# Attention's value products: high and low halves of the values in one product, and their sum on VectorE

## The chip, the cores and the metric

The kernel runs on one core of a Trainium2 chip. The metric is the device time of one launch in microseconds, as the median of three runs. A core has five engines that work beside each other, each on its own queue of instructions in order: TensorE (PE, matmuls; its weight loads are shown as PEld), VectorE (DVE), ScalarE (ACT), GpSimd (POOL) and SyncE (SP, which issues DMAs here).

## The reference, cut to what matters

A layer of three parts works on 4096 tokens of 256 channels, in float32: half a mixture-of-experts block, local attention, half a mixture-of-experts block, each behind a layer norm and with a residual.

```python
x = x + 0.5 * ffn(layernorm(x))
x = x + attn(layernorm(x))
x = x + 0.5 * ffn(layernorm(x))
```

The feed-forward part has a shared expert of 2048 hidden units and eight routed ones of 1024, two per token. The attention works in groups of 64 tokens, with 16 heads of 16 channels:

```python
att = softmax(mask(q @ k.T / sqrt(16)))     # per group of 64 tokens and head
y = att @ v                                 # the product that the change touches
out = y @ w_proj
```

## The kernel before, in words

Every float32 operand of a matmul is split into two float16 halves, a high one and a low one (what the rounding left over). A product then is three matmuls: high by high, high by low, low by high. TensorE adds them up in PSUM.

The kernel has four phases. Phase a makes the layer norm and the routing of the first feed-forward block (`tile1`, 32 tiles of 128 tokens) beside the shared expert's first four blocks of 512 tokens. Phase b runs the routed experts. Phase c runs the attention (`tile2`, 32 tiles) beside the remaining shared blocks of the first feed-forward part and most of those of the second. Phase d runs the routed experts of the second part and the last shared block.

In phase c two streams are woven together. The main stream is `shared`: for each of 16 chunks of hidden units, `gate_up` (line 363) makes 6 gate products and 6 up products of 512 columns each, into two PSUM buffers `pgu` out of three. ScalarE takes tanh of the gate (line 370), VectorE combines it with the gate (371) and with the up products (376), ScalarE rounds the result to float16 `hh` (378), and VectorE forms the low half `hl` (379). Line 371 frees the gate's buffer and line 376 the up one. The down products of a chunk (line 389: 8 with `hh`, 4 with `hl`) are issued a chunk later.

The side stream is `attn_tile`, a generator that does one step each time it is asked. `drive` with `RATE_C` = 3.0 and the class `Tiles` with `GAP_C` = 4 decide how many steps fall on each step of the main stream: a new attention tile starts every four slots, so about five are under way at once. The step that this text calls tile j's value step falls into the same slot as tile j+1's step with its scores. The order within each engine's queue is then fixed when the kernel is built: the scheduler lets each engine take the earliest written instruction that is ready on its own model of time. That is why two of a tile's value products can stand ahead of six gate products and the other thirty behind them.

The steps of an attention tile that matter here, for its 128 tokens (two groups g of 64):

- `pqk`, `pv` (line 704): query, key and value products; `vs` (605, 606) holds the values as high and low float16 halves.
- `psc` (641): the scores, 16 products of 64 columns; `S` (644) with the mask added.
- `amx` (650): the row maximum, on VectorE; line 651 subtracts it, on GpSimd, 1024 elements per partition. In the same step ScalarE copies `vs` into `V2` (655), four copies of 64x512, which double-buffers by tile.
- line 659: the exponential; 661 and 662: its high half on ScalarE, its low half on GpSimd; 665: a transposing DMA to `ET`, which has high and low of the exponential one above the other on the 128 partitions.
- the value step, `py` (673): for each g and each of 8 pairs of heads, one product with the high values and one with the low ones, 33 columns each, into the same place of PSUM. Columns 0 to 31 are the values of the pair, column 32 is ones in the high half and zeros in the low one, so that it gives the sum of the exponentials. VectorE takes the reciprocal (676) and multiplies (679), 64 rows at a time, as each half of the rows belongs to one head of the pair.
- `yp` (172 on ScalarE, 173 on GpSimd): `Y` split in two halves; two steps later its transposing DMAs `yt` (691), and two steps after that the output products `pao` (704) and the residual (697). Then comes the next layer norm with logits and, after every fourth tile, the routing.

The small products of the attention (`pqk`, `pv`, `psc`, `py`, `pao`, `pl`, `pp`) share three PSUM buffers. Lines 568 and 569 set the ones and zeros of `V2` once at the start of phase c.

Of the kernel before, what the change touches and what calls it, by code (L numbers as in the profile page):

```python
# [8 lines left out]
F32 = mybir.dt.float32  # L9
F32R = mybir.dt.float32r  # L10
F16 = mybir.dt.float16
# [4 lines left out]
ALU = mybir.AluOpType  # L16
# [4 lines left out]
P = 128  # L21
# [16 lines left out]
class Net:  # L38
# [511 lines left out]
    def attn_init(self, ln_w):  # L550
        nc = self.nc
        a = self.at
        self.lnw = a.tile([P, H], F32, name="lnw")
        nc.sync.dma_start(out=self.lnw, in_=ln_w.unsqueeze(0).to_broadcast([P, H]))
        self.mask = a.tile([P, 64], F32, name="mask")
        m2 = self.sm.tile([P, 64], F32, name="m2", bufs=1)
        for m, base in ((self.mask, 0), (m2, -64)):
            nc.gpsimd.memset(m, 0.0)
            nc.gpsimd.affine_select(
                out=m, in_=m, pattern=[[-1, 64]], compare_op=ALU.is_ge, fill=-3.0e38,  # L560
                base=base, channel_multiplier=1)
        nc.vector.tensor_copy(self.mask[64:P], m2[64:P])
        self.QK = a.tile([P, 24, P], F16, name="QK")
        nc.gpsimd.memset(self.QK, 0.0)
        self.V2 = []
        for i in range(2):
            v = a.tile([P, 2, 2, 8, 34], F16, name=f"V2{i}")
            nc.gpsimd.memset(v[:, :, 0, :, 32:33], 1.0)
            nc.gpsimd.memset(v[:, :, 1, :, 32:33], 0.0)
            self.V2.append(v)  # L570

    def attn_tile(self, R, j, x2, new_fb):

        nc = self.nc
        a = self.at
# [12 lines left out]
        V2 = self.V2[j % 2]  # L588
# [8 lines left out]
        for i in range(2):  # L597
            nc.scalar.activation(qk[:, i, :], pqk[:, i, :], AF.Square, scale=1.0 / XP, accum_out=ss[:, i:i + 1])
        nc.vector.tensor_scalar(
            out=ss, in0=ss, scalar1=XP ** 2 / H, scalar2=1e-6 * XP ** 2, op0=ALU.mult, op1=ALU.add)  # L600
# [6 lines left out]
            out=vs[:, 1, :], in0=pv, scalar=1.0 / XP, in1=vs[:, 0, :], op0=ALU.mult, op1=ALU.subtract)  # L607
        yield
        yield
        for i in range(2):  # L610
            nc.vector.scalar_tensor_tensor(
                out=qk[:, i, :], in0=pqk[:, i, :], scalar=ss[:, i:i + 1], in1=self.lnw,
                op0=ALU.mult, op1=ALU.mult)
        QS = self.QK[:, 0:16].rearrange("p (j s) (r a c) -> p j s r a c", s=2, r=2, a=4)
        for i in range(2):
            if i == 0:
                for r in range(2):
# [5 lines left out]
                        out=s[:, :, 2:4, :], in0=src, in1=s[:, :, 0:2, :], op=ALU.subtract)  # L623
            else:
# [4 lines left out]
                    out=s[:, :, 1::2, :], in0=src, in1=s[:, :, 0::2, :], op=ALU.subtract)  # L629
        yield  # L630
        QT = a.tile([P, 2, 24, 64], F16, name="QT")
        for g in range(2):
            nc.sync.dma_start_transpose(
                out=QT[:, g], in_=self.QK[g * 64:(g + 1) * 64].rearrange("p j c -> p (j c)"))
# [3 lines left out]
        for g in range(2):  # L638
            p = self.m1([P, 8, 64], F32, "psc")
            for jj in range(8):  # L640
                nc.tensor.matmul(  # L641
                    p[:, jj, :], lhsT=QT[:, g, 2 * jj:2 * jj + 2, :].rearrange("p r q -> p (r q)"),
                    rhs=QT[:, g, 16 + jj, :], start=True, stop=True)
            nc.vector.tensor_tensor(  # L644
                out=S[:, g * 8:(g + 1) * 8, :], in0=p,
                in1=self.mask.unsqueeze(1).to_broadcast([P, 8, 64]), op=ALU.add)
        yield
        mx = self.sm.tile([P, 16], F32, name="amx")
        with self.tc.issue_after(self.lows[-2]):
            nc.vector.tensor_reduce(out=mx, in_=S, axis=AX.X, op=ALU.max)  # L650
        self.anchor = nc.gpsimd.tensor_tensor(
            out=S, in0=S, in1=mx.unsqueeze(2).to_broadcast([P, 16, 64]), op=ALU.subtract)
        for g in range(2):
            for d in range(2):
                nc.scalar.copy(  # L655
                    V2[d * 64:(d + 1) * 64, g, :, :, 0:32],
                    vs[g * 64:(g + 1) * 64].rearrange("p l (j c) -> p l j c", c=32))
        yield
        nc.scalar.activation(S, S, AF.Exp, scale=0.25)
# [4 lines left out]
        ET = a.tile([P, 16, P], F16, name="ET")  # L664
        nc.sync.dma_start_transpose(out=ET, in_=e16.rearrange("p h l k -> p (h l k)"))
        yield
        yield
        Y = a.tile([P, 2, 8, 16], F32, name="Y", tag="yy")
        for g in range(2):
            py = self.m1([P, 8, 33], F32, "py")  # L670
            for jj in range(8):
                for l in range(2):
                    nc.tensor.matmul(  # L673
                        py[:, jj, :], lhsT=ET[:, g * 8 + jj, :], rhs=V2[:, g, l, jj, 0:33], start=(l == 0), stop=(l == 1))
            rc = self.sm.tile([P, 8], F32, name="rc")
            nc.vector.reciprocal(rc, py[:, :, 32])
            for r in range(2):
                sl = slice(r * 64, (r + 1) * 64)
                nc.vector.tensor_tensor(
                    out=Y[sl, g], in0=py[sl, :, r * 16:(r + 1) * 16],  # L680
                    in1=rc[sl].unsqueeze(2).to_broadcast([64, 8, 16]), op=ALU.mult)
        yield
        y = self.tok.tile([P, H], F32, name="y")
        nc.sync.dma_start(out=y, in_=R["acc"][j * P:(j + 1) * P])
        yp = a.tile([P, 2 * H], F16, name="yp")
        self.two(yp, Y.rearrange("p g j c -> p (g j c)"), True)
        yield
# [247 lines left out]
```

## Time and profile before

| what | value |
|---|---|
| median of three runs | 1791.72 us (1791.55 to 1791.86) |
| the profiled execution | 1787.42 us |
| its span | 1785.6 us |
| granted TensorE clock | 0.999 |
| value products (line 673) | 1024, from 667.9 to 1267.4 us |
| reciprocals (676) | 64, mean 179 ns |
| multiplications into Y (679) | 128, mean 287 ns |
| copies of the values (655) | 128, mean 616 ns |

The profile is of one execution. The span is the time from its first to its last instruction on the core. In the page and the groups, "128x512 f16<-128x512 f32" gives what is written and what is read, partitions by elements; "x" gives the number of instructions; behind the bar stand busy time, mean duration of one in ns, and the idle time of the engine just before these instructions with what ended it. In the lists in order of time the first number is the start, the second the duration, both in us from the start of the span, and the bracket at the end tells how long the engine had been idle and what it waited for. A matmul's duration contains the time that it takes to pass through the array; the next one starts before it ends.

### The profile page before, as it was taken

The page shows a single profiled execution, that of the slowest core. Times are in us where ns is not written, and L with a number is a line of the kernel's source. Part 1 is how long each engine was busy: PE and PEld are TensorE (multiplying, and loading weights), DVE is VectorE, ACT ScalarE, POOL GpSimd, SP SyncE. Part 2 cuts the span into 40 slices and gives each one's busy share as a digit, 9 for nine tenths or more (in the row PEclk, how much of TensorE's full clock was granted, in tenths as well). Part 3 has the DMA queues.
Part 4 walks back from the last instruction along what each step waited for, and adds up shares of the span by engine and source line. Part 5 has one row for each costly group of instructions (what it writes and reads, how often), then busy time and mean ns, then how long its engine had stood idle before and what let it go on. Part 6 is the DMA issues. An engine that isn't in the chain of part 4 may idle for free.

```text
span 1785.6 us, 37315 instructions
## 1 busy us (share of the span) xinstructions
PE 1771.0 (99%) x13652; PEld 1202.5 (67%) x13652; DVE 1198.5 (67%) x2905; ACT 945.4 (53%) x2053; POOL 757.5 (42%) x1072
## 2 busy tenths in 40 slices
PE   9999999999999999999999999999999999999998
PEld 6666667777777556666666666666666777777765
DVE  7766636666665577787778877788755566666643
ACT  5433325555554356666666666766423455555542
POOL 3777720221111345566776778676430011122210
PEclk9999999999999999999999999999999999999999
DMA  7334133555443245656557576654211144555420
GB/s 218 112 102 120 39 52 103 124 121 117 107 119 75 54 102 96 135 116 142 125 137 143 124 153 122 143 118 114 60 40 34 46 111 110 118 124 118 103 41 13
DMA packets 437544, 185.15 MB, mean 104 GB/s; under 512 B 302193, under 2 KB 434733, under 8 KB 437360
## 3 DMA queue, kind: packets, MB, share of 16 engines
q1 hardware_dynamic: 418880, 160.81, 37.8%
q0 software_dynamic: 17664, 21.17, 6.9%
q8 instruction: 107, 1.75, 0.4%
q10 hardware_dynamic: 816, 0.79, 0.1%
q14 instruction: 77, 0.63, 0.1%
HBM read 78.16 MB, written 42.21 MB: 67 GB/s over the span
## 4 chain that ended last, share of the span: by engine, by line
PE 60%; DVE 2%; ACT 2%; POOL 1%; issue 1%; DMA 1%; SPq 0%; DVEq 0%; POOLq 0%; ACTq 0%
PE pgu L363 36%; PE po L389 18%; PE pqk L704 2%; PE py L673 1%; PE pao L704 1%; PE pv L704 1%; PE psc L641 1%; DVE hl L379 1%; ACT V L655 0%; DVE sl L371 0%; DVE sl L376 0%; ACT hh L378 0%; DMA QT<-QK 0%; DVE S L644 0%; DMA xt<-xa 0%
## 5 line engine op out<-in xcount | busy, mean ns | idle before, releaser
L363 PE MATMUL pgu<-xb,sgu 128*128 128x512 f16 x3072 | 720.2, 380 | 3.4 <-DVE sl L376 2.6
L378 ACT CAST hh<-sl 128x512 f16<-128x512 f32 (+2 forms) x512 | 273.1, 534 | 487.9 <-DVE sl L376 480.6
L363 PE MATMUL pgu<-xe,wc 128*128 128x384 f16 (+1 forms) x3072 | 497.0, 299 | 0.0
L363 PEld LDWEIGHTS <-sgu 128*128 128x128 f16 x3072 | 292.9, 98 | 292.1 <-issue 5.4
L376 DVE SCALAR_TENSOR_TENSOR sl<-pgu,sl 128x512 f32<-128x512 f32 (+2 forms) x512 | 300.9, 588 | 255.0 <-PE pgu L363 228.3
L379 DVE TENSOR_TENSOR hl<-sl,hh 128x512 f16<-128x512 f32 (+2 forms) x512 | 317.4, 620 | 160.3 <-ACT hh L378 157.4
L389 PEld LDWEIGHTS <-hh 128*128 128x128 f16 x3328 | 320.5, 98 | 89.5 <-ACT hh L378 2.1
L363 PEld LDWEIGHTS <-wc 128*128 128x128 f16 x3072 | 300.6, 98 | 92.5 <-issue 0.4
L389 PE MATMUL po<-sdw,hh 128*128 128x256 f16 x2048 | 270.7, 273 | 1.3 <-ACT hh L378 1.3
L515 POOL DMA_INDIRECT out_dram<-eo,eidscatter x40 | 64.3, 1607 | 340.0 <-DVE eo L514 304.5
L374 ACT ACTIVATE sl<-pgu 128x384 f32<-128x384 f32 (+1 forms) x336 | 158.6, 473 | 79.0 <-PE pgu L363 54.5
L389 PE MATMUL po<-wd,hh 128*128 128x256 f16 x1280 | 190.3, 273 | 0.0
L515 POOL DMA_INDIRECT acc<-eo,eidscatter x40 | 65.9, 1648 | 289.7 <-DVE eo L514 253.5
L389 PEld LDWEIGHTS <-hl 128*128 128x128 f16 x1664 | 162.4, 98 | 31.6 <-DVE hl L379 1.8
L371 DVE SCALAR_TENSOR_TENSOR sl<-sl,pgu 128x512 f32<-128x512 f32 x176 | 119.9, 681 | 63.5 <-ACT sl L370 63.0
L389 PE MATMUL po<-sdw,hl 128*128 128x256 f16 x1024 | 156.9, 273 | 1.0 <-DVE hl L379 0.8
L344 POOL DMA_INDIRECT xg<-X,di x128 | 138.3, 1081 | 45.7 <-issue 28.5
L370 ACT ACTIVATE sl<-pgu 128x512 f32<-128x512 f32 x176 | 104.5, 594 | 67.1 <-PE pgu L363 60.5
L106 ACT ACTIVATE wc<-re 128x512 f16<-128x512 f32 x124 | 78.1, 630 | 73.8 <-PE pgu L363 73.7
L389 PE MATMUL po<-wd,hl 128*128 128x256 f16 x640 | 115.2, 273 | 0.0
L107 DVE SCALAR_TENSOR_TENSOR wc<-re,wc 128x512 f16<-128x512 f32 x124 | 85.7, 691 | 13.9 <-ACT wc L106 13.5
L655 ACT COPY V<-vs 64x512 f16<-64x512 f16 x128 | 78.9, 616 | 28.7 <-PE py L673 27.6
(159 smaller groups left out, 1705.4 us busy)
## 6 DMA issues: line engine op xcount, KB each, us to landing
re<-in_L_ffn_rg_dram SPq DMA_DIRECT2D x124, 128.0 KB, 2.3
re<-in_L_ffn_ru_dram SPq DMA_DIRECT2D x124, 128.0 KB, 2.5
re<-in_L_ffn_rd_dram SPq DMA_DIRECT2D x124, 128.0 KB, 2.5
y<-acc SPq DMA_DIRECT2D x64, 128.0 KB, 2.3
y<-in_L_attn_x_dram SPq DMA_DIRECT2D x32, 128.0 KB, 2.0
acc<-xr SPq DMA_DIRECT2D x16, 256.0 KB, 2.3
out_dram<-xr SPq DMA_DIRECT2D x16, 256.0 KB, 5.5
x<-y SPq DMA_DIRECT2D x28, 128.0 KB, 1.9
```

The costliest lines, as they stand in the source:

```text
L107: nc.vector.scalar_tensor_tensor(out=lo, in0=src, scalar=WS, in1=hi, op0=ALU.mult, op1=ALU.subtract)
L344: i = nc.gpsimd.indirect_dma_start(out=R["xg"][:, :], out_offset=bass.IndirectOffsetOnAxis(ap=di[:, t, k:k + 1], axis=0), in_=X, in_offset ...
L363: nc.tensor.matmul(p, lhsT=wc[:, w, i, k, :], rhs=x[:, 2 * a + k, :], start=(j == 0), stop=(j == 5))
L370: self.looks.append(nc.scalar.activation(s, p, AF.Tanh, scale=0.5 / XP).ins)
L371: nc.vector.scalar_tensor_tensor(out=s, in0=s, scalar=1.0, in1=p, op0=ALU.add, op1=ALU.mult)
L374: self.latest[0] = nc.scalar.activation(s, p, AF.Silu, scale=1.0 / XP).ins
L376: self.latest[1] = nc.vector.scalar_tensor_tensor(out=s, in0=ps[1], scalar=1.0 / XP / (2.0 * XP if tanh else 1.0), in1=s, op0=ALU.mult, op ...
L378: nc.scalar.copy(h[0], s)
L379: self.lows.append(nc.vector.tensor_tensor(out=h[1], in0=s, in1=h[0], op=ALU.subtract).ins)
L389: nc.tensor.matmul(outs[t // 2][:, (t % 2) * H:(t % 2 + 1) * H], lhsT=h[a][:, t * P:(t + 1) * P], rhs=wd[:, w], start=(c == 0 and j == 0 a ...
L515: i = nc.gpsimd.indirect_dma_start(out=R["acc"][:, :], out_offset=bass.IndirectOffsetOnAxis(ap=ids[:, t:t + 1], axis=0), in_=eo, in_offset ...
L655: nc.scalar.copy(V2[d * 64:(d + 1) * 64, g, :, :, 0:32], vs[g * 64:(g + 1) * 64].rearrange("p l (j c) -> p l j c", c=32))
```

## The change

For seven of the eight pairs of heads, high and low values now lie side by side in `V2`, so that one product of 66 columns multiplies both. Columns 0 to 32 of a pair hold the high part and the sum, columns 34 to 65 the low part. The eighth pair keeps its two products, of 33 and 32 columns, added up in PSUM[...]. ScalarE copies the low parts of the seven pairs to `yl` in SBUF; the eighth place of `yl` is zero from the start. VectorE takes the reciprocals, adds the high part from PSUM and the low part from `yl` into `Y`, and multiplies `Y` of both groups by the reciprocals in one operation at the end. A tile has 18 value products in place of 32, two more ScalarE copies, and one more VectorE operation.

```diff
@@ attn_init
-            v = a.tile([P, 2, 2, 8, 34], F16, name=f"V2{i}")
-            nc.gpsimd.memset(v[:, :, 0, :, 32:33], 1.0)
-            nc.gpsimd.memset(v[:, :, 1, :, 32:33], 0.0)
+            v = a.tile([P, 2, 8, 2, 34], F16, name=f"V2{i}")
+            nc.gpsimd.memset(v[:, :, :, :, 32:34], 0.0)
+            nc.gpsimd.memset(v[:, :, :, 0, 32:33], 1.0)
             self.V2.append(v)
+        self.yl = [a.tile([P, 8, 32], F32, name=f"yl{g}") for g in range(2)]
+        for t in self.yl:
+            nc.gpsimd.memset(t[:, 7], 0.0)
@@ attn_tile
                 nc.scalar.copy(
-                    V2[d * 64:(d + 1) * 64, g, :, :, 0:32],
+                    V2[d * 64:(d + 1) * 64, g, :, :, 0:32].rearrange("p j l c -> p l j c"),
                     vs[g * 64:(g + 1) * 64].rearrange("p l (j c) -> p l j c", c=32))
@@ attn_tile
         Y = a.tile([P, 2, 8, 16], F32, name="Y", tag="yy")
+        rc = self.sm.tile([P, 2, 8], F32, name="rc")
         for g in range(2):
-            py = self.m1([P, 8, 33], F32, "py")
-            for jj in range(8):
-                for l in range(2):
-                    nc.tensor.matmul(
-                        py[:, jj, :], lhsT=ET[:, g * 8 + jj, :], rhs=V2[:, g, l, jj, 0:33], start=(l == 0), stop=(l == 1))
-            rc = self.sm.tile([P, 8], F32, name="rc")
-            nc.vector.reciprocal(rc, py[:, :, 32])
+            py = self.m1([P, 512], F32, "py")
+            for jj in range(7):
+                nc.tensor.matmul(
+                    py[:, jj * 66:(jj + 1) * 66], lhsT=ET[:, g * 8 + jj, :],
+                    rhs=V2[:, g, jj].rearrange("p l c -> p (l c)")[:, 0:66], start=True, stop=True)
+            for l in range(2):
+                n = 33 - l
+                nc.tensor.matmul(
+                    py[:, 462:462 + n], lhsT=ET[:, g * 8 + 7, :], rhs=V2[:, g, 7, l, 0:n], start=(l == 0), stop=(l == 1),
+                    skip_group_check=True)
+            yl = self.yl[g]
+            nc.scalar.copy(yl[:, 0:7], py[:, 0:462].rearrange("p (j c) -> p j c", c=66)[:, :, 34:66])
+            hi = py[:, 0:495]
+            hi = bass.AP(hi.tensor, hi.offset, [hi.ap[0], [66, 8], [1, 33]])
+            nc.vector.reciprocal(rc[:, g], hi[:, :, 32])
             for r in range(2):
                 sl = slice(r * 64, (r + 1) * 64)
-                nc.vector.tensor_tensor(
-                    out=Y[sl, g], in0=py[sl, :, r * 16:(r + 1) * 16],
-                    in1=rc[sl].unsqueeze(2).to_broadcast([64, 8, 16]), op=ALU.mult)
+                c = slice(r * 16, (r + 1) * 16)
+                nc.vector.tensor_tensor(out=Y[sl, g], in0=hi[sl, :, c], in1=yl[sl, :, c], op=ALU.add)
+        nc.vector.tensor_tensor(
+            out=Y, in0=Y, in1=rc.unsqueeze(3).to_broadcast([P, 2, 8, 16]), op=ALU.mult)
```

## The prediction

> **What bounds the kernel now.** I read the page's first part, then the table by stage, the groups of instructions inside the attention stage, and last the instructions in order of time around one attention tile.
>
> The page, busy time of each engine:
> ```profile
> PE 1771.0 (99%) x13652; PEld 1202.5 (67%) x13652; DVE 1198.5 (67%) x2905; ACT 945.4 (53%) x2053; POOL 757.5 (42%) x1072
> ```
> A busy TensorE proves little here, since the ends of its matmuls are modelled. What counts is whether it ever waits. The value products run from 667.9 to 1267.4 us, so I took four consecutive attention tiles of that stretch (columns: length, then busy time of each engine, clock, DMA):
> ```profile
> core 0: us, PE busy (x) PEld busy (x) DVE busy (x) ACT busy (x) POOL busy (x), PEclk, DMA share, GB/s
> 1034.30:1112.80 78.50, 78.50 (x671) 50.25 (x670) 62.89 (x164) 53.15 (x112) 58.72 (x81) 1.00 0.68 136
> ```
> A tile takes 78.5/4 = 19.6 us. VectorE is busy 80% of it, ScalarE 68%, GpSimd 75%, at full clock. The groups of 745 to 1245 us (last column: idle time of the engine before them):
> ```profile
> L363 PE MATMUL pgu<-xb,sgu 128*128 128x512 f16 x1230 | 289.0, 379 | 0.0
> L379 DVE TENSOR_TENSOR hl<-sl,hh 128x512 f16<-128x512 f32 x103 | 78.6, 763 | 26.1 <-ACT hh L378 25.7
> L679 DVE TENSOR_TENSOR Y<-py,rc 64x128 f32<-64x128 f32 x104 | 29.8, 286 | 1.5
> L673 PE MATMUL py<-V,ET 128*128 128x33 f16 x800 | 25.3, 177 | 0.0
> L673 PEld LDWEIGHTS <-ET 128*128 128x128 f16 x800 | 25.0, 96 | 6.5
> L641 PE MATMUL psc<-QT 128*128 128x64 f16 x404 | 18.5, 193 | 0.0
> ```
> No matmul group waited at all in 500 us, while VectorE waits for ScalarE and ScalarE for VectorE. TensorE's own issue spacing therefore sets the time, and a spacing taken out of its stream shortens the run one for one, until another engine falls behind its slack.
>
> **The change part by part. TensorE.** The 177 ns of a value product is latency; the cost is the distance from start to start:
> ```profile
> 1048.26 0.40 PE L641 MATMUL psc<-QT 128*128 128x64 f16 x8
> 1048.49 2.75 PE L363 MATMUL pgu<-xb,sgu 128*128 128x512 f16 x12
> ...
> 1052.63 2.75 PE L363 MATMUL pgu<-xb,sgu 128*128 128x512 f16 x12
> 1055.22 0.96 PE L673 MATMUL py<-V,ET 128*128 128x33 f16 x32
> 1056.03 0.60 PE L389 MATMUL po<-sdw,hh 128*128 128x256 f16 x4
> ```
> 32 value products of 33 columns take 1056.03 - 1055.22 = 0.81 us, 25.3 ns each, loads included. 8 products of 64 columns take 0.23 us, 28.8 ns each; 12 of 512 take 2.59 us, 215.8 each. Between the last two a column costs 0.417 ns, so 66 columns cost 28.8 + 0.8 = 29.6 ns. A tile then needs 14 x 29.6 + 4 x 25.3 = 515 ns in place of 810: 0.295 us less, 9.4 us in 32 tiles. The bounds of the new form are near: at 28.8 ns it would be 9.8 us; at twice 25.3 (no gain from width) nothing. The row of 64 columns, with a fresh load for each product as here, is the nearest, so I keep 29.6.
>
> A rule would give far more. The Trainium skill, "TensorE: Matmul & The Clock Gate", section "LDWEIGHTS (loading the stationary operand)", prices a weight load at its columns divided by 1.2 per ns, 107 ns for 128. If loads were the bound, 14 fewer per tile would save 1.5 us, 48 us in all. The row has loads of 96 ns, but 25.3 ns apart: they overlap. I go by the spacing.
>
> **ScalarE** gets two copies per tile, 128x224 from PSUM. Near rows, both from PSUM: 372 ns for 256 elements (L598), 167 for 16 (L238); between them 345 ns. That makes 0.69 us per tile, ScalarE at (53.15/4 + 0.69)/19.3 = 72%. The copies stand where ScalarE idles for the value products anyway (1.15 us ahead of the V copies below). Queued behind them are those V copies and then the cast hh of line 378, for which VectorE's hl and the down products wait.
>
> **VectorE** keeps two reciprocals (179 ns) and four operations of 64x128 with one operand in PSUM; the second operand is now yl instead of rc, and I price them at the same 286 (230 to 296 in the trace, so 0.2 us per tile either way at most). New is one multiplication of 128x256 from SBUF. The nearest row is L173 on VectorE, 128x256 with two SBUF inputs: 417 ns. VectorE comes to (62.89/4 + 0.42)/19.3 = 84%. New is also a wait: the additions wait for ScalarE's copies, and the reciprocals may stand behind these too. If each copy follows its products as the V copies do now (0.09 us after them), the second ends about 0.45 us after the last product. In the four tiles the first Y operation starts 0.5 to 2.9 us after that product, its reciprocal 0.2 us earlier, so the wait costs from nothing to 0.3 us, and 0.7 if both copies come late. I take nothing, as three of the four start later than 1 us.
>
> **The multiplication and GpSimd.** The old Y operations had one SBUF operand; the multiplication has two. A rule speaks against that: "SBUF — State Buffer", section "Summary: rules for kernel authors", says that a VectorE instruction with two SBUF inputs and a GpSimd one that reads SBUF exclude each other; the second to issue waits for the first to end. Three engines in order of time, at two tiles:
> ```profile
> 1042.26 2.13 POOL L662 TENSOR_TENSOR e<-S,e 128x1024 f16<-128x1024 f32 x1 [0.83 <-ACT e L661]
> 1043.73 1.22 DVE L379 TENSOR_TENSOR hl<-sl,hh 128x512 f16<-128x512 f32 x1
> ...
> 1075.45 2.50 ACT L655 COPY V<-vs 64x512 f16<-64x512 f16 x4 [1.15 <-PE py L673]
> 1076.24 1.21 DVE L679 TENSOR_TENSOR Y<-py,rc 64x128 f32<-64x128 f32 x4
> 1076.57 1.92 POOL L651 TENSOR_TENSOR S<-S,amx 128x1024 f32<-128x1024 f32 x1
> 1078.62 0.69 DVE L379 TENSOR_TENSOR hl<-sl,hh 128x512 f16<-128x512 f32 x1 [1.17 <-ACT hh L378]
> ```
> The trace agrees: hl takes 0.69 us when free, but 1.22 when it meets GpSimd's operation, and it ends 0.56 us after that. In the tile of 1076 us the multiplication would come at 1077.45, into S of line 651, which ends at 1078.49: 1.04 us of waiting. Of the four tiles, S is already over in two when Y ends (1039.19 against 1039.66; 1099.11 against 1100.50), in the third it ends within the last 0.05 us (1058.43, 1058.47). By the row alone VectorE pays 0.42 us per tile; by the rule 0.42 to 2.4 (the whole of S ahead), 0.7 on average with this order.
>
> Who waits for that? Behind Y stand hl and the next gate's line 371. VectorE then idles, 0.57 to 1.17 us before hl or 0.83 to 1.06 before line 371, in three of the four tiles; this is cover. The fourth (1099 us) has none. The hard limit is TensorE: each group of gate or up products needs the PSUM buffer of the group three before. From start times in the trace, group start minus the end of the VectorE operation that freed its buffer: least 0.38 us, 1.16 at the fifth percentile, median 1.8; in the fourth tile 1.64 for the group at 1103.87. The down products come at least 0.6 us after hh and 0.75 after hl, medians 2.2 and 1.8. A delay of 0.4 to 1.1 us per tile passes into this slack, and TensorE pays nothing in the steady part. Without the cover, each 0.1 us of stall per tile costs 3.2 us.
>
> **What else moves.** Y comes 0.4 to 1.5 us later; yp, its two transposes on SP's queue and the output products follow two and four steps later (the next output product starts at 1079.39 for a Y of 1058.47, the transposes take about 4), so the DMAs stay covered. In the fourth tile ScalarE waits for Y already (0.34 us), with the next tanh behind it; that is inside the 1.64. The order on SP's and GpSimd's queues is not changed by hand. At the start of the stage GpSimd gets two more memsets and wider ones (0.16 to 0.19 us each before, around 599 us): under 1 us beside a stage whose first value product comes 68 us later, taken as nothing. The V copies write runs of 32 values as before: 617 ns kept.
>
> **Sum.** From 640 to 745 us, with about five tiles, TensorE was busy 102.29 of 105 us: it waits there for others, so a shorter stream need not end sooner. I count two of these five tiles as lost, 0.6 us. 9.4 - 0.6 = 8.8 us. The profiled execution, 1787.42 us (span 1785.6), would be 1778.6. It lies 0.24% under the median of 1791.72; against that the forecast is 1782.9.
>
> **The rivals.** Measurement tells about 0.2%, 3.6 us, from no change.
> *Full gain* (0.69): 1782.9, own range 1781 to 1787.
> *Cover partly used up* (0.11): the instruction order of each engine is made anew at build time, and the V copies and hh move by 0.69 us. If hl or a buffer comes 0.2 us late per tile, 6.4 of 8.8 us go: 1789.3. For it: least slacks of 0.4 to 0.75; against it: medians of 1.8. That the width isn't free (66 columns cost as two times 33) would give 1791.7; the 64-column row speaks against it.
> *VectorE held in front of the gate buffers* (0.20): the additions wait for both copies (0.69) and the multiplication for all of S (1.95 + 0.42), together 3.06 us ahead of line 371. Less 0.83 idle and 1.81 slack, 0.42 us stay per tile, 13.4 in all: 1796.3, slower. It decides from 0.28 us of stall per tile, a delay of about 2.9 us. For it: three engines at 70 to 84% that wait for each other in order; against it: it needs all of S behind Y's end in every tile, where this order has it in one of four.
>
> **How the numbers follow.** Faster 0.69 (the full gain), same 0.11, slower 0.20. The range goes from 1781 (9.8 us saved and a little of the early waits) to 1796, which leaves out less than 0.04 below and about half of the slower case above.
>
> **What would show it.** In the profile after: 448 products of 66 columns and 128 of 32 or 33, the former about 29.6 ns apart; a tile of 19.3 us; no idle time before L363, L389 or the products; copies of about 345 ns; a multiplication of 0.42, or longer by what S still has to run. I am wrong if TensorE shows waits for lines 371, 376, 378 or 379 in each tile, or if the value products are spaced near 50 ns.

## The result, and the profile after

The changed kernel takes 1800.58 us (median of six runs, 1797.19 to 1801.29); the kernel before took 1791.63 us in the runs beside it. The ratio is 1.005, with a 95% interval of 1.004 to 1.006: 9 us slower, where 9 us faster were forecast. The profiled execution took 1800.25 us, its span is 1798.5 us, its clock 0.999.

The page's first part, then one period of four attention tiles, from the tile behind one routing tile to the tile behind the next (columns as in the table by stage of before):

```profile
PE 1768.3 (98%) x13204; PEld 1193.7 (66%) x13204; DVE 1229.6 (68%) x2937; ACT 959.9 (53%) x2117; POOL 764.8 (43%) x1074
```

```profile
1042.64:1123.96 81.32, 78.46 (x614) 49.12 (x613) 68.35 (x168) 54.76 (x120) 59.44 (x81) 1.00 0.69 131
```

Before, the four tiles took 78.50 us and TensorE was busy in all of it. Now they take 81.32, and TensorE is idle for 2.86 us of them, at an unchanged clock. VectorE's work has grown by 5.5 us per four tiles; the forecast had four multiplications of 0.42, 1.7 us. The groups of 745 to 1245 us show where the rest is (line numbers are now those of the changed kernel: lines 598 to 668 of before are 3 higher now, so 651 is 654 and 662 is 665; 704 is 717):

```profile
L379 DVE TENSOR_TENSOR hl<-sl,hh 128x512 f16<-128x512 f32 x99 | 88.3, 892 | 12.8 <-ACT hh L378 12.2
...
L693 DVE TENSOR_TENSOR Y<-Y,rc 128x256 f32<-128x256 f32 x25 | 14.6, 583 | 0.8
...
L294 DVE SCALAR_TENSOR_TENSOR df<-ef,pos 128x8 f32<-128x8 f32 x6 | 13.4, 2230 | 0.0
```

All three read two operands from SBUF. Line 379 has gone from 763 to 892 ns on average, the new multiplication takes 583, and line 294, a step of the routing on 8 elements per partition, takes 2.23 us. Of VectorE's operations in that stretch I took those that lasted over 0.1 us longer than the median of their kind (for line 294, its undisturbed 0.16 us). Together they took 38.8 us more than that median, against 15.7 us before; line 379 has 20.1 us of it (7.3 before), line 294 12.4 (7.5), the multiplication 4.0.

TensorE's waits, over the whole span (columns: waiting group, what it waited for, us in total, times, longest):

```profile
PE pao L717 <- DVE Y L692: 6.3, 5, 1.3
PE psc L644 <- DVE qk L614: 3.3, 5, 0.7
...
PE pqk L717 <- DVE Y L692: 2.1, 5, 0.5
```

The largest is in none of the places that the prediction had looked at. The output products `pao` and the next tile's `pqk` wait for the additions into `Y`, since these free the PSUM buffers of the value products, and `pao`, `pqk` take the same three buffers. It happens five times: in five of the six routing tiles of that stretch (in a routing tile, one of four, the steps of the routing run beside the attention's). `psc` waits for line 614 in the same tiles, and `pgu` for line 371 nine times in the same 500 us (1.6 us). One of the waits for `Y` in order of time, from all engines:

```profile
944.65 0.98 POOL L344 DMA_INDIRECT xg<-X,di  x1 [0.30 <-issue]
945.19 2.40 DVE L294 SCALAR_TENSOR_TENSOR df<-ef,pos 128x8 f32<-128x8 f32 x1
945.63 1.93 POOL L654 TENSOR_TENSOR S<-S,amx 128x1024 f32<-128x1024 f32 x1
...
947.64 0.54 DVE L692 TENSOR_TENSOR Y<-py,yl 64x128 f32<-64x128 f32 x2
948.32 0.82 PE L717 MATMUL pao<-wpr,yt 128*128 128x256 f16 x6 [1.25 <-DVE Y L692]
948.81 0.17 DVE L300 CAST di<-df 128x8 int32<-128x8 f32 x1 [0.23 <-DMA xg<-X,di]
949.12 0.54 DVE L692 TENSOR_TENSOR Y<-py,yl 64x128 f32<-64x128 f32 x2
949.80 1.46 PE L717 MATMUL pqk<-wqkv,xt 128*128 128x512 f16 x6 [0.45 <-DVE Y L692]
```

Read it from the second line. `df` of line 294 begins at 945.19 while GpSimd is in a scatter, and it is not done until 947.59, 0.03 us after GpSimd's subtraction into `S`. The first group's reciprocal and additions stand behind it in VectorE's queue and end at 948.18; `pao`, which has waited 1.25 us, starts 0.14 us later. Then two more routing steps and `di`, which waits 0.23 us for a DMA, come between the first and the second group's additions, and `pqk` waits for these. Before, at the same tile:

```profile
940.29 1.93 POOL L651 TENSOR_TENSOR S<-S,amx 128x1024 f32<-128x1024 f32 x1
940.66 1.59 DVE L294 SCALAR_TENSOR_TENSOR df<-ef,pos 128x8 f32<-128x8 f32 x1
...
942.41 1.21 DVE L679 TENSOR_TENSOR Y<-py,rc 64x128 f32<-64x128 f32 x4
...
943.50 0.82 PE L704 MATMUL pao<-wpr,yt 128*128 128x256 f16 x6
```

The same hold was there, 1.59 us long, and it too ended with `S` (942.25 and 942.22). The four operations that free both buffers ran together right behind it, and `pao` did not wait.

The wait of `psc` in the same tile comes from the opposite case, a GpSimd operation behind one of VectorE:

```profile
935.36 0.68 DVE L379 TENSOR_TENSOR hl<-sl,hh 128x512 f16<-128x512 f32 x1
935.43 1.19 POOL L604 TENSOR_TENSOR ss<-ss,mhalf 128x2 f32<-128x2 f32 x1
...
936.66 0.88 DVE L614 SCALAR_TENSOR_TENSOR qk<-pqk,ss,lnw 128x256 f32<-128x256 f32 x2 [0.62 <-POOL ss L604]
...
937.68 0.39 PE L644 MATMUL psc<-QT 128*128 128x64 f16 x8 [0.66 <-DVE qk L614]
```

`ss` takes 0.70 us as a median, and 1.19 here, where `hl` began 0.07 us ahead of it; in all five tiles with this wait it takes 1.19 to 1.20, always with `hl` just ahead. Line 614 waits for `ss`, and `psc` for line 614, which frees the buffer of `pqk`.

**Where the time went, as a sum.** For each pair of successive matmuls I took the distance from start to start and subtracted what the columns of the first one cost when TensorE is never held up. That cost is read from the trace of before, where the median distance is 216 ns for 512 columns, 109 for 256, 29 for 64 and 25 for 33: columns divided by 2.4, plus 2.5 ns, and at least 25.5 ns. With it the kernel before has a remainder of -0.2 us between 745 and 1245 us. The sum of these costs is called TensorE's work, the sum of the remainders its waits.

| kernel, profiled execution | work, us | waits in the whole span | of these 745 to 1245 us |
|---|---|---|---|
| before | 1761.8 | 17.6 | -0.2 |
| after | 1752.4 | 40.0 | 19.7 |

The work follows from the numbers of columns alone, so its fall by 9.4 us is a calculation. Measured from start to start, the value products took 26.5 us before (0.5 of it two waits) and 17.3 after, 8.7 us less without the waits. The waits grew by 22.4, of which 19.9 in the steady part. The difference, 13.0 us, is that of the two profiled executions (12.8). The medians differ by 9 us, because the profiled execution of before lies 4.2 us under the median of its runs.

Of the 19.7 us, counted in this way (the list above counts from the modelled end of the product before, and so less), `pao` has 7.1 and `pqk` 2.9, 10.0 us for the buffers of the value products; `psc` has 5.0, the gate and up products 3.3, the down products that wait for `hl` 1.2.

### The profile page after: what moved, and what is told of

Its sections match the earlier page's. It is cut to its first block, busy times and chain, and to the rows that moved or that the text cites. A ratio compares the mean times of both kernels' runs of the same rounds, so it can differ in the third digit from the quotient of the medians.

```text
span 1798.5 us, 36515 instructions
## 1 busy us (share of the span) xinstructions
PE 1768.3 (98%) x13204; PEld 1193.7 (66%) x13204; DVE 1229.6 (68%) x2937; ACT 959.9 (53%) x2117; POOL 764.8 (43%) x1074
## 4 chain that ended last, share of the span: by engine, by line
PE 48%; DVE 7%; POOL 5%; ACT 4%; issue 2%; DMA 1%; DVEq 0%; POOLq 0%; SPq 0%; ACTq 0%
PE pgu L363 29%; PE po L389 15%; DVE hl L379 1%; PE pqk L717 1%; DVE sl L376 1%; DVE sl L371 1%; POOL S L654 1%; DVE df L294 1%; POOL ss L604 1%; ACT hh L378 1%; ACT V L658 1%; PE pv L717 1%; POOL xg L344 1%; PE pao L717 1%; ACT S L662 1%
## 5 line engine op out<-in xcount | busy, mean ns | idle before, releaser
L379 DVE TENSOR_TENSOR hl<-sl,hh 128x512 f16<-128x512 f32 (+2 forms) x512 | 329.1, 643 | 143.7 <-ACT hh L378 135.4
L344 POOL DMA_INDIRECT xg<-X,di x128 | 134.1, 1047 | 45.8 <-issue 28.6
L370 ACT ACTIVATE sl<-pgu 128x512 f32<-128x512 f32 x176 | 104.4, 593 | 45.3 <-PE pgu L363 38.5
```

The source lines that it names most:

```text
L344: i = nc.gpsimd.indirect_dma_start(out=R["xg"][:, :], out_offset=bass.IndirectOffsetOnAxis(ap=di[:, t, k:k + 1], axis=0), in_=X, in_offset ...
L370: self.looks.append(nc.scalar.activation(s, p, AF.Tanh, scale=0.5 / XP).ins)
L379: self.lows.append(nc.vector.tensor_tensor(out=h[1], in0=s, in1=h[0], op=ALU.subtract).ins)
```

## The theories, and what the runs were to tell apart

*The hold theory*: TensorE's saving is real, and it is lost since VectorE frees the value products' buffers too late, mostly in the routing tile, where operations with two SBUF operands are held by GpSimd (in the expectations theory A, with variants A1 and C, and the exclusion theory). *The first rival*: 66-column products cost more than forecast, so that little was saved. *The second rival* (A2 there): the added work itself (two copies, one multiplication, the wait for the copies) costs what was lost, wherever it stands. *The third rival* (theory B there): the order of the instructions, made anew with every build, makes the loss by itself. No run holds the order fixed, so none of them excludes this one.

In all that follows a ratio is to the kernel before on the same chip, with its 95% interval; "waits" is the sum explained above. An expected time in us is to be read against the 1791.6 us of the kernel before that it starts from. The edits are cut to the lines that matter.

### The parts by themselves: e1_products_only, e2_evacuation_only

The first keeps the 66-column products and drops the copies and additions, so that the low part of the values is left out for seven of eight pairs:

```diff
-            nc.scalar.copy(yl[:, 0:7], py[:, 0:462]...)
-                nc.vector.tensor_tensor(out=Y[sl, g], in0=hi[sl, :, c], in1=yl[sl, :, c], op=ALU.add)
-        nc.vector.tensor_tensor(
-            out=Y, in0=Y, in1=rc.unsqueeze(3).to_broadcast([P, 2, 8, 16]), op=ALU.mult)
+                nc.vector.tensor_tensor(out=Y[sl, g], in0=hi[sl, :, c],
+                    in1=rc[sl, g].unsqueeze(2).to_broadcast([64, 8, 16]), op=ALU.mult)
```

> The changed kernel's 18 value products per tile with the evacuation of the kernel before: no copies to yl, Y is the high part times the reciprocal straight from PSUM. Left out: the low part of the values for seven of eight pairs. Before 1791.6, changed 1800.6 us. Theory A (TensorE's saving is real, 9 us, and is lost to the new evacuation, which in the routing tile holds the value products' PSUM buffers): 1782.6, within 2 us. Theory B (the gain was never there, or the newly made instruction order alone makes the loss): 1791 to 1801.

Measured: 0.9972 (0.9961 to 0.9984), 5 us faster, where the hold theory had expected 9; waits 19.9 us for 17.6, 1.0 in the steady part. A period of four tiles takes 77.3 us for 78.5, 0.30 us less per tile, as forecast. The first rival falls.

The second keeps the 32 products of before and puts the new evacuation behind them (the copy multiplies by zero, so that the sum stays what it was):

```diff
+            yl = self.yl[g]
+            nc.scalar.mul(yl[:, 0:7], py[:, 0:7, 0:32], 0.0)
...
-                nc.vector.tensor_tensor(
-                    out=Y[sl, g], in0=py[sl, :, r * 16:(r + 1) * 16],
-                    in1=rc[sl].unsqueeze(2).to_broadcast([64, 8, 16]), op=ALU.mult)
+                nc.vector.tensor_tensor(out=Y[sl, g], in0=py[sl, :, c], in1=yl[sl, :, c], op=ALU.add)
+        nc.vector.tensor_tensor(
+            out=Y, in0=Y, in1=rc.unsqueeze(3).to_broadcast([P, 2, 8, 16]), op=ALU.mult)
```

> The opposite half: the 32 value products of the kernel before, with the changed kernel's evacuation (two ScalarE copies of 128x224, here scaled by zero so that the sum stays as it was, additions, one multiplication at the end). Theory A: slower than before by the full loss of the evacuation, 1805 to 1810 us, with TensorE idle ahead of the output and key products of every fourth tile. Theory B: near 1792, as nothing of the product stream is changed.

Measured: 1.002 (1.0013 to 1.0028), 3.6 us slower; waits 21.3 us, 1.0 in the steady part. The hold theory as put there, with the whole loss coming from the evacuation (1805 to 1810 us, a ratio of 1.0075 to 1.010), was wrong. The added work costs 3.6 us beside the old products, the shorter stream gives 5.0, and the two together would give -1.4. They give +9. So the second rival falls as well, as far as it means a cost that does not depend on the products: 10 us come only from the two together. In this run's routing tile `df` runs free (0.16 us), and the routing's next step, `pos`, is held in its place, though it has one operand:

```profile
943.55 1.92 POOL L654 TENSOR_TENSOR S<-S,amx 128x1024 f32<-128x1024 f32 x1
943.64 1.87 DVE L296 TENSOR_SCALAR pos<-pos 128x8 f32<-128x8 f32 x1
```

The routing tile near 940 us shows how the slack was used up. Times count from the start of the last value product; TensorE starts 0.14 us after an addition's end when it has waited for it.

| kernel | GpSimd's S ends | Y of group 0 ends, pao starts | Y of group 1 ends, pqk starts |
|---|---|---|---|
| before | 2.96 | 3.74, 4.24 | 4.36, 5.11 |
| e1, products alone | 3.30 | 4.08, 4.34 | 4.70, 5.00 |
| e2, evacuation alone | 3.85 | 4.45, 4.60 | 5.53, 5.68 |
| after, both | 5.00 | 5.61, 5.75 | 7.09, 7.24 |

Before had 0.36 and 0.61 us to spare (start minus end, less 0.14). In the other three tiles of a period the least was 2.1 us. The products alone leave 0.12 and 0.16, the evacuation alone 0.01 and 0.01. Each part uses up nearly all the slack and costs TensorE about 0.2 us per routing tile at most; both together overdraw it. This is not the whole of why the parts don't add up: the first end of `Y` comes 0.34 us later with the one, 0.71 with the other and 1.87 with both, since `S`, which it follows, comes 2.04 us later for 0.34 and 0.89.

### The hold taken away: e4_df_gpsimd, x2_halves, x3_halves_df, x4_halves_df_pos

`e4` moves `df` and its second step (294, 298) to GpSimd:

```diff
-        nc.vector.scalar_tensor_tensor(
-            out=df, in0=ef, scalar=float(CAP), in1=pos, op0=ALU.mult, op1=ALU.add)
+        nc.gpsimd.tensor_scalar_mul(df, ef, float(CAP))
+        nc.gpsimd.tensor_tensor(out=df, in0=df, in1=pos, op=ALU.add)
...
-        nc.vector.tensor_tensor(out=df, in0=df, in1=pos, op=ALU.add)
+        nc.gpsimd.tensor_tensor(out=df, in0=df, in1=pos, op=ALU.add)
```

> The changed kernel with the routing's two additions that make df (lines 294 and 298, two SBUF inputs each, tiny) moved from VectorE to GpSimd. In the changed kernel the first lasts 2.40 us on VectorE, until GpSimd's subtraction of the row maximum ends, and the additions into Y stand behind it. Theory A1 (df, locked out by GpSimd, holds the value products' PSUM buffers): at least the 10 us of TensorE's waits ahead of the output and key products go, 1783 to 1791. Theory A2 (load of VectorE and ScalarE): 1798 to 1801, as df is 8 operations of little work.

Measured: 1.0026 (1.0016 to 1.0036), between the two ranges expected; waits 33.2 us, 12.4 in the steady part. The additions end at 3.84 and 4.68 us after the last product, `pao` and `pqk` start at 4.89 and 5.77: neither waits any more, although `S` now ends at 5.60. With `df` out of VectorE's queue their 10.0 us are gone, but only 7.3 us left the sum, as other waits came in their place (`psc` 4.2 us for line 609, the down products 2.9 for `hl`).

`x2` leaves `df` where it is and cuts GpSimd's two long subtractions (654, 665) into two operations over eight heads each, so that a held instruction is let in earlier (the first of the two is shown):

```diff
-        self.anchor = nc.gpsimd.tensor_tensor(
-            out=S, in0=S, in1=mx.unsqueeze(2).to_broadcast([P, 16, 64]), op=ALU.subtract)
+        for i in (0, 8):
+            self.anchor = nc.gpsimd.tensor_tensor(
+                out=S[:, i:i + 8], in0=S[:, i:i + 8], in1=mx[:, i:i + 8].unsqueeze(2).to_broadcast([P, 8, 64]), op=ALU.subtract)
```

> The changed kernel with GpSimd's two large operations of the softmax (subtraction of the maximum, low half of the exponential) each split into two of 512 elements, so that a VectorE instruction that meets one waits half as long. By durations above the median, VectorE is held 38 us in the 500 us from 745 to 1245 in the changed kernel and 16 in the one before. Theory A1 (exclusion between VectorE and GpSimd makes the loss): the held time falls by a third or more, and the time to 0.997 to 1.001 of before. Theory B (the newly made order alone): no such relation, 1.003 to 1.007.

Measured: 1.0016 (1.0009 to 1.0023), between the two ranges again; waits 28.7 us, 12.1 in the steady part. But not for the reason given: the held time, which was to fall by a third or more, fell from 38.8 to 33.2 us, and `df` still took 2.54 us, straight through both halves (they end at 3.58 and 4.57 after the last product, the first additions at 5.18), and `pao` and `pqk` wait as before, 5.7 and 2.1 us in all. What went are the waits for lines 614 and 371.

`x3` is both edits in one; `x4` moves `pos` (296) to GpSimd as well:

> The split of GpSimd's two operations, and df's two additions on GpSimd, both in the changed kernel. With the split alone TensorE's steady waits were those ahead of the output and key products of each routing tile (9.4 us in the 500), where df is held for 2.38 us and the additions stand behind it. Theory A1 (those waits are df's): they go, and TensorE's saving comes through: 0.995 to 0.998 of before. Theory A2 (load): 1.000 to 1.003, as with the split alone.

> As the one with split and df on GpSimd, with the routing's comparison (line 296, one SBUF input) on GpSimd too, since such a line was held for 1.87 us where df got through, in the run with the new evacuation alone. Theory A1: 0.995 to 0.998, the same or a little better. Theory A2: 1.000 to 1.003.

Measured: 1.0002 (0.9993 to 1.001) and 1.0001 (0.9992 to 1.001), both short of what the hold theory expected and within what A2, the load of the added work, would give (1.000 to 1.003). In `x4` the additions end at 3.04 and 3.88, `pao` and `pqk` start at 4.24 and 5.11, the places that they had before, with more slack than before. The steady waits are 7.9 us, and one kind leads:

```profile
PE po L389 <- DVE hl L379: 5.3, 11, 0.6
```

So `pao` and `pqk` no longer wait, and the kernel is as fast as before, not faster: the 9.4 us of work are saved, and waits of 9.3 us (26.9 less 17.6) stand against them. Between 745 and 1245 us ten waits for `hl` take 6.3 us, five of each of two kinds. In one `hl` is held by GpSimd again (950.83 to 952.22, 1.40 us for 0.69, with GpSimd's line 631 until 951.67). In the other it takes its 0.68 us and comes late because two operations of line 422 and one of 647 stand ahead of it. So the second half of these waits is a matter of VectorE's load or order and not of a hold, and which of the two was not tested.

The same edits on the kernel before, as a control:

> Control: the kernel before with the same split of GpSimd's two operations. TensorE had no waits to lose there, so all theories of the changed kernel's loss expect 0.998 to 1.001; more than 1.002 would mean that the split itself, or any newly made order, costs time.

> Control: both edits in the kernel before. TensorE has no steady waits there: 0.998 to 1.001 by every theory. What the combination gains below this is TensorE's saving alone.

Measured: 0.9996 (0.999 to 1.0003) and 0.9989 (0.9983 to 0.9996), with no steady waits in either (0.0 and -0.2 us). The halves take 0.34% off the changed kernel (1.0016 against 1.005) and 0.04% off the one before, halves and `df` together 0.48% and 0.11% (the first ratio of each pair is from another chip than the second): nearly all that they remove are waits that the changed kernel has and the one before has not. `c3` is the fastest kernel here that does the whole computation, 2 us faster than before, and it is without the change.

### Other places: e3_mult_gpsimd, x1_copies_first

`e3` puts the new multiplication on GpSimd (`nc.vector.tensor_tensor` becomes `nc.gpsimd.tensor_tensor` in the last operation of the diff):

> The changed kernel with the final multiplication of Y by the reciprocals moved from VectorE to GpSimd, which takes 0.42 us per tile off VectorE. Theory A1 (the loss is the place of the additions in VectorE's queue, not its load): the multiplication frees no buffer, so 1797 to 1801. Theory A2 (VectorE's added 13 us of work are the loss): 1788 to 1793.

Measured: 1.0061 (1.0044 to 1.0078); steady waits 18.2 us for 19.7, `pao` 6.2 and `pqk` 2.1 as before. The second rival had 1788 to 1793 us here, a ratio of 0.998 to 1.001, and this speaks against it. The multiplication on VectorE, which the prediction spent most of its care on, is not where the time goes; it stands behind the additions that free the buffers.

`x1` holds ScalarE's copies of `vs` back behind the last copy of `yl`:

> The changed kernel with an order edge on ScalarE: the V copies of the next tile stand behind both yl copies. In the changed kernel two V copies (1.25 us) lie between the two yl copies, the second reciprocal waits for the second copy, and so the second PSUM buffer of the value products is held longer. Theory A3 (what holds that buffer is ScalarE's order): TensorE's wait ahead of the key products goes and VectorE's additions follow each other; 1.000 to 1.003 of before (the changed kernel is 1.005). Theory A1 (VectorE is held by GpSimd, the copy is long there when VectorE comes): no change, 1.004 to 1.007.

Measured: 1.0208 (1.0191 to 1.0225), far from both ranges. The whole order was made anew: `pl` waits 12.9 us for a DMA of `xb`, the value products 5.5 for `ET`. It tells nothing of the copies. The trace of the changed kernel tells more; this is the copy of the second group in the routing tile shown above:

```profile
944.02 0.35 ACT L685 COPY yl<-py 128x224 f32<-128x224 f32 x1
```

It is done at 944.37, and the first reciprocal starts at 947.52, the second at 949.00. So in that tile the copies did not hold VectorE up. Whether another place for them would have led to a better order stays open.

### More time for the attention: the runs with RATE_C at 3.1 and 3.2

`RATE_C` sets how many steps of the attention fall on a step of the main stream, and a greater number spreads the same GpSimd and VectorE work over more of TensorE's. `x6` and `c6` are the changed kernel and the one before at 3.2, `x9` and `c9` at 3.1; `x10` is `x9` with the edits of `x3`.

> The changed kernel with RATE_C 3.2 in place of 3.0: a slot of attention and routing steps comes every 3.2 steps of the shared expert's stream, so that GpSimd and VectorE have 7% more time for an attention tile; the amount of work is the same. Theory C (in the routing tile GpSimd's chain, 93 to 96% busy, keeps its length of about 18 us, and a shorter TensorE stream runs into it): TensorE's waits in the 500 us from 745 fall from 20 us to under 5, and the time to 0.995 to 0.999 of before. Theory B (the newly made order alone): 1.002 to 1.007, as any other order.

> Control: the kernel before with RATE_C 3.2. It has no steady waits to lose, so 0.998 to 1.002 by theory C; what the changed kernel gains below this at the same rate is TensorE's saving.

> The changed kernel with RATE_C 3.1 in place of 3.0. Exclusion theory (GpSimd and VectorE each get 3% more time per attention tile): TensorE's waits between 745 and 1245 us fall from 19.7 to between 8 and 14 us, and the expert load of the second routed part is late by about half of what 3.2 showed (0 to 7 us); 1787 to 1795, below c9_before_rate31. A fixed cost of the added operations instead: waits of 19 to 20 us as before, and not below c9_before_rate31.

> The kernel before with RATE_C 3.1. It had no waits in the steady part, so a slower attention gives it nothing: 1791 to 1799, as the expert load of the second routed part comes later.

> The changed kernel at RATE_C 3.1, with GpSimd's two long subtractions in halves and df on GpSimd. Exclusion theory: hardly a wait for the value products' PSUM buffers is left, TensorE's waits between 745 and 1245 us are under 6 us, and the time is below x9_rate31 by 2 to 6 us. If the waits were those of the added ScalarE copies, it would be no faster than x9_rate31.

| kernel | ratio | waits in the whole span | 745 to 1245 us |
|---|---|---|---|
| x6, after at 3.2 | 1.0032 (1.002 to 1.0045) | 38.5 | 7.2 |
| c6, before at 3.2 | 1.0071 (1.0054 to 1.0088) | 35.2 | 2.8 |
| x9, after at 3.1 | 1.0031 (1.0019 to 1.0043) | 39.3 | 19.0 |
| c9, before at 3.1 | 1.0049 (1.0035 to 1.0062) | 32.1 | 17.7 |
| x10, after at 3.1, halves and df | 0.9998 (0.9989 to 1.0007) | 32.1 | 12.4 |

At 3.2 the steady waits fall to 7.2 us, as the theory has it, though under 5 were expected, and at the same rate the changed kernel is the faster one by 0.4%. The times of both lie above what was expected, 1.0032 for 0.995 to 0.999 and 1.0071 for 0.998 to 1.002: each loses 12 us once where the attention, ending later, keeps the second routed part waiting for its first tokens, `xe`. At 3.1 the theory failed as I had put it: the waits stay at 19.0 us where 8 to 14 were expected, and the kernel before, for which none were expected, has 17.7; both times are above their ranges too. So waits of this size need no change of the products; another order is enough, and the third rival stands. `x10` kept 12.4 where under 6 were expected, and is 6 us (0.33%) faster than `x9`, for 2 to 6 expected.

`x9` shows something else, VectorE in order of time and the TensorE group that waits:

```profile
1132.10 2.35 DVE L693 TENSOR_TENSOR Y<-Y,rc 128x256 f32<-128x256 f32 x1
...
1134.48 0.69 DVE L371 SCALAR_TENSOR_TENSOR sl<-sl,pgu 128x512 f32<-128x512 f32 x1
...
1135.22 1.46 PE L363 MATMUL pgu<-xb,sgu 128*128 128x512 f16 x6 [0.86 <-DVE sl L371]
```

Here the multiplication of 0.42 us takes 2.35, because GpSimd's line 665 runs from 1131.76 to 1134.17; line 371 stands behind it, and the gate products wait 0.86 us. This is the slower rival to the letter, in an order in which the multiplication is held for 10.5 us between 745 and 1245 us, against 4.0 in the changed kernel.

## Why the prediction was wrong, point by point

- **TensorE's saving: right.** 9.4 us were forecast, and the value products' distances shrank by 8.7. The 448 products of 66 columns are spaced 30.9 ns on average, 257 of them 29 or 30, for 29.6 forecast; the 64 of 33 columns 29.0 for 25.3. The row of 64 columns was the right one to price by, and the price of 1.5 us per tile for weight loads was rightly set aside.
- **The durations: right.** A copy takes 345 ns for 345, a multiplication that nothing holds 0.42 for 0.42, the additions 269 ns for 286.
- **The multiplication and GpSimd: the mechanism right, the amount smaller.** It was held for 4.0 us in 25 tiles, 0.16 per tile, where the rule's average was put at 0.28 over its own 0.42.
- **"TensorE pays nothing in the steady part": this step failed, and it decides the sign.** It paid 19.7 us, 10.0 of them ahead of `pao` and `pqk`. Slack was measured for the buffers of the gate and up products, for `hh` and for `hl`. It was not measured for the buffers of the value products themselves, though the change lengthens just their release: a copy before the additions, and the additions of both groups no longer back to back. The trace of before had the number, 0.36 and 0.61 us in every routing tile from 860 us on. The prediction set delays of 0.4 to 1.1 us against medians of 1.8 us for other buffers; and even those were not free, with 3.3 us for the gate and up products and 1.2 us for `hl`, at the same one or two places of every period of four tiles. There the least slack counts, not the median.
- **The fourth tile.** The prediction noted that it has no cover, took for it the slack of one gate group alone (1.64 us), and let the other three decide. All waits for the value products' buffers are in the routing tile, one of four. A wait of 2 us in every fourth tile costs what 0.5 in each would.
- **What is held.** The rule of the Trainium skill ("SBUF — State Buffer", "Summary: rules for kernel authors") was priced for the operation that the change adds and not for those that stood there: `hl` and `df` are bound by it too, and `df`, held for 1.59 us in the trace of before with the reciprocals behind it, was not in the sum. The trace bears the rule out, and adds that a held operation need not be large: one of 8 elements per partition took 2.40 us.
- **The rivals.** The slower one, at 1796.3, was given 0.20. It had the kind of cause (VectorE held by GpSimd ahead of a PSUM buffer) and half the loss, 4.6 us for 9, and the place wrong: `df` for the multiplication, `py`'s buffers for the gate's. Its point against ("it needs all of S behind Y's end in every tile") holds for the multiplication alone.

What stays open: why `S` of GpSimd ends at 5.00 us after the last value product in the changed kernel and at 3.85 or less with either part alone. Counted from the routing's first step on VectorE (line 251), its end comes 18.83 us later, for 18.14 before, and the last product 13.84 for 15.18; both moved. The order of each queue is made anew with every edit, and no run here holds it fixed, so how much of the loss belongs to the change and how much to the order that it happened to get is not shown. Nor is it settled what would bring the 9 us through: in `x4` `pao` and `pqk` do not wait, but the down products still wait for `hl`, which they do not in `c3`.

## What to carry to other kernels

Before pricing a change at what TensorE saves, list every buffer whose release the change touches, and take for each the least slack over one whole period of the pattern, not the median: a tile that comes every fourth time decides. Look there for small operations that the trace shows far above their size, and ask what stands behind them. Two parts that each fit into the same slack need not fit together, so a part measured alone at no cost proves little.

## What the runs showed of the hardware that was not expected

- A VectorE operation that waits for GpSimd can be passed by GpSimd's next one, as I read the records. `df` began to wait at 945.19 during a scatter that ended at 945.63; the subtraction that followed started at 945.63 and ran its 1.93 us, and only then `df` was done. In `x2` it took 2.54 us, through the rest of a scatter and two subtractions: shorter GpSimd operations with no gap between them let nothing in there.
- An operation with a single SBUF operand of 8 float32 per partition (`pos`) was held too, 1.87 us where 0.11 is its duration in the trace of before.
- The hold works both ways: `ss` on GpSimd, 2 elements per partition, took 1.19 us in place of 0.70 behind VectorE's `hl`.
- A 66-column product with a fresh load of 128x128 costs 30.9 ns on average from start to start, a 33-column one of the kernel before 25.3: doubling the columns costs about a fifth more.
